# Gate and up of a gated feed-forward as seven block products, with one PSUM bank for projections and tails

## The chip, the cores and the metric

The kernel runs on one core of one Trainium2 chip. The metric is the device time of one execution in microseconds; the number given for a kernel is the median of several executions. A profile is one execution recorded by the hardware profiler; its span runs from the first to the last instruction. Engines: PE is TensorE (matmul; PEld its weight loads), DVE is VectorE, ACT is ScalarE, POOL is GpSimd, SP issues most of the DMAs. Each engine works off its own instructions in order.

## What is computed

All values are f32. x is [8, 256, 512]; eight batches of 256 tokens, 512 features. First a windowed cross-attention with 32 heads is added (q from context and normed x, k and v from each), then a feed-forward:

```python
x = x + tanh(g_xattn[0]) * attention(layernorm(x), ctx, Wq, Wk, Wv, Wsk, Wsv, Wo)
xt = layernorm(x)                                        # feed-forward from here
topk_p, topk_idx = top_k(softmax(xt @ w_router), 4)      # 128 experts
gate, up = (xt @ w_gate).reshape(T, 8, 256), (xt @ w_up).reshape(T, 8, 256)
basis = silu(gate) * up                                  # 8 bases of 256
mixed = sum over the 4 chosen experts e and the bases k of coeff[e] * mix[e, k] * basis[k]
out = mixed @ w_down + (silu(xt @ shared_w_gate) * (xt @ shared_w_up)) @ shared_w_down
x = x + tanh(g_ffn[0]) * out
```

The down projection is linear, so the kernel sums the experts' mixing weights per token first (one coefficient per token and base) and multiplies by w_down once.

## The kernel before

A batch has four pieces of work, each a Python generator that emits instructions and yields a cost after each step:

- `project` (L253): loads x and context, norms x, transposes it, and computes k, q (four groups of 16 matmuls) and v. Each result goes through a PSUM bank and is evicted by ScalarE (L289, L306, L322).
- `attention` (L329): scores on TensorE (L355, four banks, one for each pair of head groups), bias and maximum on VectorE (L368, "softmax rows" here), exponential on ScalarE (L377), division on GpSimd (L387), 32x32 transposes on VectorE (L395), value matmuls on TensorE (L417) into the rest of the same banks, eviction by ScalarE (L434).
- `tail` (L495), for each half of the tokens: output projection (L504), residual, norm, transposition into hT, router (L528), top-4 selection, coefficients `cf`.
- `feed_forward` (L572): for each of four pieces of two bases and for each half t of the tokens, four matmuls of 512 columns for gate and four for up (L589). Tanh on ScalarE (L600) and an STT on VectorE (L601) make silu, L606 multiplies by up, L611 and L613 add the two bases to `mixed[t]`. VectorE's later part of a piece (`late`) is emitted only after the next piece's gate matmuls. Then come the shared part (L630, four steps), and the down projections (L665, L670).

Order: nothing is scheduled by a planner; the loop `run` (L690) always continues the generator with the smallest virtual time, which advances by the yielded cost times a rate chosen at `start`. So the instructions of attention b+1, projection b+2 and the feed-forward of b alternate on each engine in a fixed order. While b is 0, projections and attention are emitted by hand (L705 to L719).

PSUM has eight banks of 2 KB per partition: four for scores and values (`ps_sc`), one for projections (`ps_pj`), one for tails (`ps_tl`), two for the feed-forward (`ps_gu`). Weights of gate and up are loaded anew for each batch, one piece of two bases (1 MB for gate, 1 MB for up) two pieces ahead (`load_gu`, L237, called after a piece's last matmul at L619 and L659), through SP's queue. Waits between engines are put in by the framework from the tiles that instructions touch.

Of the kernel before, what the change touches and what calls it, by code (L numbers as in the profile page):

```python
# [9 lines left out]
F32 = mybir.dt.float32  # L10
# [18 lines left out]
NK2 = NK // 2  # L29
# [8 lines left out]
def gated_block(  # L38
# [28 lines left out]
    three = ctx.enter_context(tc.tile_pool(name="three", bufs=3))  # L67
    small = ctx.enter_context(tc.tile_pool(name="small", bufs=4))
    PS = bass.MemoryType.PSUM
    ps_sc = ctx.enter_context(tc.tile_pool(name="ps_sc", bufs=4, space=PS))  # L70
    ps_pj = ctx.enter_context(tc.tile_pool(name="ps_pj", bufs=1, space=PS))
    ps_tl = ctx.enter_context(tc.tile_pool(name="ps_tl", bufs=1, space=PS))
    ps_gu = ctx.enter_context(tc.tile_pool(name="ps_gu", bufs=2, space=PS))
# [4 lines left out]
    def load(b):  # L78
        xt = three.tile([P, NT, HID], F32, tag="x", name=f"x_{b}")
        ctT = two.tile([P, NC, T], F32, tag="ctT", name=f"ctT_{b}")  # L80
        nc.sync.dma_start(xt, x[b].rearrange("(t p) d -> p t d", p=P))
        nc.sync.dma_start(ctT, context_t[b].rearrange("(c p) t -> p c t", p=P))
        loaded[b] = xt, ctT
# [6 lines left out]
    load(0)  # L90
# [10 lines left out]
    load(1)  # L101
# [59 lines left out]
    dist = const.tile([P, NW * Q], F32, tag="dist", name="dist")  # L161
# [36 lines left out]
    def other_weights():  # L198
# [11 lines left out]
        nc.sync.dma_start(escale, expert_scale.rearrange("(e o) -> e o", o=1))  # L210
        later["wr"] = weight(w_router, HID, E, "wr", nc.sync)
        load_gu(0)
        load_gu(1)
# [20 lines left out]
    wgu = {}  # L234
    PIECES = NK2 + 1

    def load_gu(i):  # L237
        if i >= B * PIECES:
            return
        k2 = i % PIECES  # L240
        for name, routed, shared in (("wg", w_gate, sw_gate), ("wu", w_up, sw_up)):
            t = two.tile([P, NC, 2 * I], F32, tag=name, name=f"{name}_{i}")
            src = routed[:, k2 * 2 * I : (k2 + 1) * 2 * I] if k2 < NK2 else shared
            nc.sync.dma_start(t, src.rearrange("(c p) n -> p c n", p=P))
            wgu[name, i] = t
# [4 lines left out]
    AFTER, BEFORE = 2.0, 1.6  # L250
    projected = {}

    def project(b):  # L253
        def bank(shape, name):

            pool, tag = (ps_gu, "gu") if b < 2 else (ps_pj, "pj")
            return pool.tile(shape, F32, tag=tag, name=name)

        if b > 1:
            load(b)  # L260
            yield 24.0
# [9 lines left out]
        for t in range(NT):  # L271
            evict = transposed(xnT, xns[t], t, f"x{b}", bank)
            yield AFTER
            evict()
            yield BEFORE


        kT = two.tile([P, 2, 2, T], F32, tag="kT", name=f"kT_{b}")
        pk = bank([P, 2, T], f"pk_{b}")
# [7 lines left out]
        for par in range(2):  # L287
            for s in range(2):
                nc.scalar.activation(  # L289
                    kT[:, par, s, :], pk[:, s, :], AF.Copy, scale=kmask[:, par : par + 1],  # L290
                )
        yield BEFORE
# [3 lines left out]
        for g in range(G):  # L296
            pq = bank([P, T], f"pq_{b}_{g}")
# [10 lines left out]
            )  # L308
            yield BEFORE
        projected[b] = kT, qT  # L310


        pv = bank([P, NT, 2, HK * D], f"pv_{b}")
# [11 lines left out]
        )  # L325
        yield BEFORE


    def attention(b):  # L329
# [112 lines left out]
        for u in range(2 * n + 4):  # L442
# [27 lines left out]
            for step, ps in enumerate(((0,), (1, 2), (3,))):  # L470
# [3 lines left out]
                if step == 1 and j == 1 and m is not None:  # L474
                    take(m, scs)
                    if m == n // 4 - 1:
                        start(tail(b, 0, oT), 0.37, total=37.0)
# [11 lines left out]
        start(tail(b, 1, oT), 0.37 if b > 0 else 0.30, total=37.0)  # L489
# [4 lines left out]

    def tail(b, t, oT):  # L495
        def bank(shape, name):
            return ps_tl.tile(shape, F32, tag="tl", name=name)
# [3 lines left out]
        yield 2.0  # L501
        po = bank([P, HID], f"po_{n}")
# [9 lines left out]
        )  # L512
        normed = norm(xt, [t], f"f{b}")
# [5 lines left out]
        hT = hTs[b]  # L519
        evict = transposed(hT, xn, t, f"f{b}", bank)  # L520
        yield 3.0
        evict()
# [241 lines left out]
```

## Time and profile before

| | |
|---|---|
| time, median of 3 | 1091.81 us (1088.89 to 1093.41) |
| profiled execution | 1087.13 us |
| its span | 1085.4 us |
| granted TensorE clock, mean | 0.991 |
| PE busy | 1050.7 us, 97% |
| DVE, ACT, POOL busy | 524.1, 347.2, 228.8 us |
| gate and up matmuls (L589), busy | 465.7 us |
| DMA moved | 120.78 MB |

A line of a group names line, engine, operation, the tile written <- the tiles read, the shape, the number of rows, busy time and mean duration. Each f32 matmul of the code is recorded as two rows. A wait line names who waited for whom: microseconds in total, how often, the longest. A chain line gives start, length and what ran. Busy time of an engine is the union of its rows, so rows that overlap in the pipeline count once; the mean duration of a matmul is longer than the distance of two neighbours.

### The profile page before, as it was taken

Reading aid. Unit: us, or ns where it says so; the run is one execution under the profiler, and the core shown is the slowest. Engines: PE = TensorE matmul, PEld = TensorE weight load, DVE = VectorE, ACT = ScalarE, POOL = GpSimd, SP = SyncE. Lnnn points to the kernel's source line nnn. Section 1 sums busy time; section 2 is a strip of 40 time slices with the busy share of each in tenths; the row PEclk is TensorE's granted clock in tenths of the full one; section 3 lists DMA queues with packets and bytes.
Section 4 is the critical chain, followed back from the end, with each engine's and each line's share of the span. In section 5 each row is a group of like instructions: output and inputs, shape, how many; then the busy total and the mean of one; then the engine's idle time right before and its main releaser. Section 6 shows DMA issues by size and latency. Waiting matters only on the chain.

```text
span 1085.4 us, 23220 instructions
## 1 busy us (share of the span) xinstructions
PE 1050.7 (97%) x9232; PEld 646.2 (60%) x9232; DVE 524.1 (48%) x1952; ACT 347.2 (32%) x1354; POOL 228.8 (21%) x587
## 2 busy tenths in 40 slices
PE   7988999999999999999999999999999999999998
PEld 6765465844658446675566745676455754565445
DVE  1564652536526265353744445444563536663431
ACT  1552442414423134232432224332442314431100
POOL 3342221203212032121312112221221212321000
PEclk9899999999999999999999999999999999999999
DMA  9803421127212462135522254222632236322330
GB/s 304 269 2 78 138 98 57 43 96 216 88 69 71 139 200 79 40 115 127 170 78 78 90 127 156 79 78 89 175 109 77 79 113 166 132 79 99 118 114 19
DMA packets 75132, 120.78 MB, mean 111 GB/s; under 512 B 4624, under 2 KB 27664, under 8 KB 75024
## 3 DMA queue, kind: packets, MB, share of 16 engines
q1 hardware_dynamic: 72912, 117.47, 34.6%
q10 hardware_dynamic: 2112, 1.84, 0.5%
q8 instruction: 72, 1.18, 0.5%
q14 instruction: 36, 0.29, 0.1%
HBM read 98.31 MB, written 4.19 MB: 94 GB/s over the span
## 4 chain that ended last, share of the span: by engine, by line
PE 91%; DVE 6%; ACT 1%; issue 1%; DMA 0%; POOL 0%; DVEq 0%; ACTq 0%
PE gu L589 37%; PE pq L299 10%; PE ps L630 10%; PE sc L417 6%; PE sc L355 6%; PE po L504 5%; PE pd L670 5%; PE pk L282 3%; PE pv L317 3%; PE pd L665 2%; PE pl L528 1%; DVE pt L395 1%; DVE pr L368 1%; ACT pr L377 1%; DVE st_a L115 1%
## 5 line engine op out<-in xcount | busy, mean ns | idle before, releaser
L377 ACT ACTIVATE pr<-pr,nm 128x192 f32<-128x192 f32 (+2 forms) x512 | 218.2, 427 | 475.6 <-DVE rd L384 296.6
L387 POOL TENSOR_SCALAR pr<-pr,rd 128x192 f32<-128x192 f32 (+2 forms) x512 | 205.4, 422 | 582.1 <-DVE rd L384 559.3
L368 DVE CUSTOM_DVE_ANT_1 pr<-sc,nbias 128x192 f32<-128x192 f32 (+2 forms) x512 | 148.8, 324 | 244.4 <-PE sc L355 139.5
L589 PE MATMUL gu<-wu,hT 128*128 128x512 f32 x512 | 232.3, 596 | 1.4 <-DVE th L606 1.4
L589 PE MATMUL gu<-wg,hT 128*128 128x512 f32 x512 | 233.4, 598 | 0.0
L589 PEld LDWEIGHTS gu<-wu,hT 128*128 128x128 f32 x512 | 94.6, 190 | 107.6 <-issue 100.1
L589 PEld LDWEIGHTS gu<-wg,hT 128*128 128x128 f32 x512 | 94.6, 190 | 104.4 <-issue 101.5
L395 DVE STREAM_TRANSPOSE pt<-pr 128x768 f32<-128x768 f32 (+2 forms) x128 | 111.5, 871 | 0.9 <-POOL pr L387 0.8
L601 DVE SCALAR_TENSOR_TENSOR th<-th,gu 128x512 f32<-128x512 f32 x64 | 44.0, 688 | 110.4 <-ACT th L600 110.4
L377 ACT ACTIVATION_READ_ACCUMULATOR pr<-pr,nm 128x1 f32 x512 | 96.1, 188 | 0.0
L417 PEld LDWEIGHTS sc<-pt,vbd 64*32 64x32 f32 x5120 | 61.3, 107 | 25.7 <-issue 20.9
L417 PE MATMUL sc<-pt,vbd 64*32 64x96 f32 (+2 forms) x5120 | 68.8, 231 | 5.0 <-issue 3.0
L355 PE MATMUL sc<-kT,qT 32*128 32x192 f32 (+2 forms) x1024 | 67.4, 342 | 3.0 <-DVE nm L368 2.7
L355 PEld LDWEIGHTS sc<-kT,qT 32*128 32x128 f32 x1024 | 47.6, 187 | 33.1 <-issue 22.3
L299 PE MATMUL pq<-ctT,wq 128*128 128x256 f32 x256 | 61.4, 383 | 2.8 <-ACT qT L306 2.8
L299 PE MATMUL pq<-xnT,wq 128*128 128x256 f32 x256 | 61.9, 385 | 0.0
L606 DVE TENSOR_TENSOR th<-th,gu 128x512 f32<-128x512 f32 x64 | 43.1, 673 | 37.9 <-PE gu L589 37.7
L630 PE MATMUL ps<-hT,wg 128*128 128x256 f32 x256 | 61.2, 382 | 0.0
L630 PE MATMUL ps<-hT,wu 128*128 128x256 f32 x256 | 60.5, 379 | 0.0
L504 PE MATMUL po<-wo,oT 128*128 128x512 f32 x128 | 58.2, 597 | 1.9 <-DVE cf L567 1.9
L299 PEld LDWEIGHTS pq<-ctT,wq 128*128 128x128 f32 x256 | 47.9, 190 | 19.4 <-issue 8.6
L670 PE MATMUL pd<-sd,shT 128*128 128x512 f32 x128 | 58.3, 597 | 0.3 <-DVE shT L643 0.3
(96 smaller groups left out, 880.9 us busy)
## 6 DMA issues: line engine op xcount, KB each, us to landing
wg<-in_L_ffn_w_gate SPq DMA_DIRECT2D x32, 1024.0 KB, 4.9
wu<-in_L_ffn_w_up SPq DMA_DIRECT2D x32, 1024.0 KB, 5.0
vbd<-vpad SPq DMA_DIRECT2D x128, 128.0 KB, 3.2
wg<-in_L_ffn_shared_w_gate SPq DMA_DIRECT2D x8, 1024.0 KB, 5.0
wu<-in_L_ffn_shared_w_up SPq DMA_DIRECT2D x8, 1024.0 KB, 5.4
x<-in_x SPq DMA_DIRECT2D x8, 512.0 KB, 3.8
ctT<-in_ctx SPq DMA_DIRECT2D x8, 512.0 KB, 5.1
out<-x SPq DMA_DIRECT2D x16, 256.0 KB, 2.1
```

The lines of the kernel that those rows point to most:

```text
L299: nc.tensor.matmul(pq, lhsT=wq_sb[:, c, g * P : (g + 1) * P], rhs=(ctT if c < NC else xnT)[:, c % NC, :], start=(c == 0), stop=(c == 2 * N ...
L355: nc.tensor.matmul(seen(scs[p][:, j * COLS : (j + 1) * COLS], qb), lhsT=qT[rows, qb].rearrange("p g q -> p (g q)"), rhs=kT[rows, par, :, f ...
L368: nc.vector.tensor_tensor_reduce(out=part, in0=seen(scs[p][:, j * COLS : (j + 1) * COLS], qb0 + j), in1=bass.AP(tensor=bias.tensor, offset ...
L377: nc.scalar.activation(part, part, AF.Exp, bias=nmax[:, p : p + 1], scale=-1.0, accum_out=den[:, p : p + 1],)
L387: nc.gpsimd.tensor_scalar(part, part, rden[:, p : p + 1], 1.0, op0=ALU.mult, op1=ALU.mult)
L395: nc.vector.transpose(pt[:, u % 4].rearrange("p c (s k) -> p (c s) k", s=2)[:, :, lo:], pr.rearrange("p c (s k) -> p (c s) k", s=2)[:, :, ...
L417: nc.tensor.matmul(scs[gp][32 * c : 32 * (c + 1), 2 * COLS + lo * Q : 2 * COLS + hi * Q], lhsT=vbd[rows, kb % (P // Q), kb // (P // Q) * 2 ...
L504: nc.tensor.matmul(po, lhsT=oT[:, ch // 2, ch % 2, t * P : (t + 1) * P], rhs=wo_sb[:, ch % 2, ch // 2, :], start=(ch == 0), stop=(ch == 3),)
L589: nc.tensor.matmul(gate if up is None else up, lhsT=hT[:, c, t * P : (t + 1) * P], rhs=w_sb[:, c, :], start=(c == 0), stop=(c == NC - 1),)
L601: nc.vector.scalar_tensor_tensor(out=th, in0=th, scalar=1.0, in1=gate, op0=ALU.add, op1=ALU.mult)
L630: nc.tensor.matmul(pg[:, j, :], lhsT=wgu[name, i][:, c, ic * P : (ic + 1) * P], rhs=hT[:, c, :], start=(c == 0), stop=(c == NC - 1),)
L670: nc.tensor.matmul(po, lhsT=shT[:, ic, t * P : (t + 1) * P], rhs=later["sd"][:, ic, :], start=False, stop=(ic == NSI - 1),)
```

## The change

For batches 1 to 7, gate and up of one base are computed together. With tokens split in halves (A, rows of the left matrix), features split in halves (the sum over 512), and B the 512 x 512 matrix whose left columns are the base's gate weights and whose right columns are its up weights, the product is a 2 x 2 by 2 x 2 block product. Strassen's scheme in Winograd's form takes seven block products of (128 tokens) x (256 features) x (256 columns), each two matmuls of 256 columns, for eight. It needs sums of blocks of tokens, sums of blocks of weights, and sums of results:

- Token sums: `token_sums`, four VectorE rows for each batch, issued in the tail.
- Weight sums: batch 0 multiplies as before (`plain`, in halves of gate and up for one base), and GpSimd makes the sums of the weights meanwhile (`weight_sums`, `last_sum`). SP stores blocks and sums in DRAM (`scratch`), from which later batches load seven blocks of 256 KB a base, two bases ahead.
- Result sums: partly in PSUM by accumulation. ScalarE copies the first product into another bank (`seeded`), and later products add to it; the rest is added by VectorE (`second_up`, `rest`). `seeded` is one bank of two halves, used in turn by even and odd bases; `pair0` and `pair1` hold a base each. A matmul at the start of the run writes all of `seeded` once.
- Bases are staggered: 1 and 5 of base k, then 7 of base k-1, 2 and 6 of base k, 3 and 4 of base k-1. The last base's rest lies within the shared part's first step.
- `mixed` and the silu rows are now of 256 columns, one for each base and half. Shared weights are loaded in two parts, and mixed's transposes for both halves go through one bank.
- Projections, tails and `mixed`'s transposes use one bank (`ps_one`) with a flag `held`: a generator that wants the bank while another has it yields until it is free. Batch 0 and 1 project through the pairs.
- The context tile and `prob` have one buffer, context is loaded later; the rates and costs of the generators are other ones, and attention of the next batch starts 0.15 batch earlier.

```diff
+    pair = [ps_gu.tile([P, 2, T], F32, tag=f"pair{j}", name=f"pair{j}") for j in range(2)]
+    seeded = ps_gu.tile([P, 2, T], F32, tag="seeded", name="seeded")
...
+    def hold():
+        while held[0]:
+            yield 0.4
+        held[0] = True
...
+        loaded[1] = x_1, load_context(1)
         later["wr"] = weight(w_router, HID, E, "wr", nc.sync)
-        load_gu(0)
-        load_gu(1)
+        for i in range(2):
+            for g in range(1, 5):
+                load_gu(i, g)
...
+        elif b == 0:
+            src = (w_gate, w_gate, w_up, w_up)[g - 1]
+            rows = slice(HALF, HID) if g in (2, 4) else slice(0, HALF)
+            nc.sync.dma_start(
+                t[:, 0], src[rows, k * I : (k + 1) * I].rearrange("(c p) n -> p c n", p=P)
+            )
+        else:
+            nc.sync.dma_start(t, scratch[k, g])
+
+    def after(i, g):
+
+        b, k = divmod(i, PIECES)
+        if g < 3:
+            load_gu(i + 2, g)
+        else:
+            load_gu(i + 2 if k < NK - 2 else (b + 1) * PIECES + k - NK + 2, g)
...
+        sT = one.tile([P, 4, NC // 2, P], F32, tag="sT", name=f"sT_{b}")
+        a11, a12 = hT[:, : NC // 2, :P], hT[:, NC // 2 :, :P]
+        a21, a22 = hT[:, : NC // 2, P:], hT[:, NC // 2 :, P:]
+        nc.vector.tensor_add(sT[:, 0], a21, a22)
+        nc.vector.tensor_sub(sT[:, 1], sT[:, 0], a11)
+        nc.vector.tensor_sub(sT[:, 2], a11, a21)
+        nc.vector.tensor_sub(sT[:, 3], a12, sT[:, 1])
...
+        def weight_sums(k):
+
+            w = [wgu[k, g] for g in range(1, 5)]
+            nc.gpsimd.tensor_sub(w[0][:, 1], w[2][:, 0], w[0][:, 0])
+            nc.gpsimd.tensor_sub(w[1][:, 1], w[3][:, 0], w[0][:, 1])
+            nc.gpsimd.tensor_sub(w[3][:, 1], w[1][:, 0], w[1][:, 1])
+            for g in (1, 2, 4):
+                nc.sync.dma_start(scratch[k, g], w[g - 1])
+
+        def last_sum(k):
+
+            w = [wgu[k, g] for g in range(1, 5)]
+            nc.gpsimd.tensor_sub(w[2][:, 0], w[3][:, 0], w[2][:, 0])
+            nc.sync.dma_start(scratch[k, 3], w[2])
...
+            for k, t in order:
+                plain(k, t)
+                while len(todo) > 1:
+                    todo.pop(0)()
+                while len(ths) > 3:
+                    mix_in(*next(iter(ths)))
+                if t == 0:
+                    weight_sums(k)
+                yield 3.46
+                if t == 1:
+                    last_sum(k)
+                    for g in range(1, 5):
+                        after(k, g)
...
+            def product(k, m, dst, first=False):
+                g, j = weights_of[m]
+                w = wgu[b * PIECES + k, g]
+                for c in range(NC // 2):
+                    nc.tensor.matmul(
+                        dst, lhsT=sides_of[m][c], rhs=w[:, j, c, :],
+                        start=(first and c == 0), stop=(c == NC // 2 - 1),
+                        skip_group_check=True,
+                    )
+
+            def one_and_five(k):
+                banks[k] = next_pair()
+                product(k, 1, banks[k][:, 0, :], first=True)
+                product(k, 5, banks[k][:, 1, :])
+                after(b * PIECES + k, 1)
+
+            def seed(k):
+                nc.scalar.copy(seeded[:, k % 2, :], banks[k][:, 0, :])
+                ups[k] = three.tile([P, I], F32, tag="up", name=f"up_{b}_1_{k}")
+                nc.scalar.copy(ups[k], banks[k][:, 1, :])
+
+            def two_and_six(k):
+                product(k, 2, banks[k][:, 0, :])
+                product(k, 6, seeded[:, k % 2, :])
+                after(b * PIECES + k, 2)
+
+            def first_gate(k):
+                us[k] = two.tile([P, I], F32, tag="u", name=f"u_{b}_{k}")
+                nc.scalar.copy(us[k], seeded[:, k % 2, :])
+                ths[k, 0] = silu2(banks[k][:, 0, :], f"th_{b}_0_{k}")
+
+            def seven(k):
+                product(k, 7, seeded[:, k % 2, :])
+                after(b * PIECES + k, 3)
+
+            def second_up(k):
+                nc.vector.tensor_add(ups[k], ups[k], seeded[:, k % 2, :])
+
+            def three_and_four(k):
+                product(k, 3, banks[k][:, 1, :])
+                product(k, 4, seeded[:, k % 2, :])
+                after(b * PIECES + k, 4)
+
+            def rest(k):
+                up = three.tile([P, I], F32, tag="up", name=f"up_{b}_0_{k}")
+                nc.vector.tensor_add(up, us.pop(k), banks.pop(k)[:, 1, :])
+                ths[k, 1] = silu2(seeded[:, k % 2, :], f"th_{b}_1_{k}")
+                nc.vector.tensor_mul(ths[k, 0], ths[k, 0], up)
+                nc.vector.tensor_mul(ths[k, 1], ths[k, 1], ups.pop(k))
+
+
+            for k in range(NK):
+                one_and_five(k)
+                if k > 1:
+                    for t in range(NT):
+                        mix_in(k - 2, t)
+                yield 1.73
+                seed(k)
+                if k > 0:
+                    seven(k - 1)
+                    yield 0.86
+                    second_up(k - 1)
+                two_and_six(k)
+                yield 1.73
+                first_gate(k)
+                if k > 0:
+                    three_and_four(k - 1)
+                    yield 1.73
+                    rest(k - 1)
...
         for b in range(B):
+            if b + 1 < B:
+                run(b + EARLY)
+                start(attention(b + 1), 0.86, at=b + EARLY, total=71.0)
             run(float(b) if b > 0 else -0.1)
-            start(feed_forward(b), b + 1.0 - now[0], total=80.5)
-            if b + 1 < B:
-                start(attention(b + 1), 0.90, at=b + 0.01, total=71.0)
+            start(feed_forward(b), b + 1.0 - now[0], total=73.2 if b > 0 else 80.6)
             if b + 2 < B:
-                start(project(b + 2), 0.73, at=b + 0.005, total=71.0)
+                start(project(b + 2), 0.62, at=b + 0.01, total=60.0)
```

`silu2(gate, name)` is a tanh of 256 columns on ScalarE and an STT on VectorE, (tanh + 1) * gate; `mix_in(k, t)` is one VectorE row of 256 columns, which adds a base to `mixed[t]`.

## The prediction

> **What bounds the kernel now.** I read the page's busy shares first, then a table of stages, then the chain that ended last, then TensorE's waits.
>
> ```profile
> PE 1050.7 (97%) x9232; PEld 646.2 (60%) x9232; DVE 524.1 (48%) x1952; ACT 347.2 (32%) x1354; POOL 228.8 (21%) x587
> ...
> PE 91%; DVE 6%; ACT 1%; issue 1%; DMA 0%; POOL 0%; DVEq 0%; ACTq 0%
> ```
>
> ```profile
> 533.00:666.00 133.00, 131.85 (x1232) 81.13 (x1230) 66.50 (x248) 43.56 (x171) 27.75 (x69) 1.00 0.36 113
> ```
>
> TensorE is busy 97% of the span and 131.85 of 133 us in the middle (columns: length, then PE, PEld, DVE, ACT, POOL, clock, DMA share, GB/s). The chain is 91% TensorE. A batch takes 130.4 us (the same stretch of shared products starts at 469.66, 600.03, 730.53 and 860.93 us in the chain). The granted clock is 1.00 there, so clock explains nothing. Only less TensorE work, or more TensorE waiting, moves the time. Two stretches of the chain give the pitch of a matmul:
>
> ```profile
> 1022.56 34.44 PE gu L589 x80
> 1056.99 6.91 PE ps L630 x32
> ```
>
> 80 rows of 512 columns in 34.44 us are 0.430 us each, 32 rows of 256 columns in 6.91 us 0.216 us each (each f32 matmul of the code is two rows). Half the columns cost half the time, so small blocks lose nothing by themselves: the weight load, 190 ns, still fits under 216. The mean durations of 598 and 382 ns on the page are latencies of overlapping rows and may not be multiplied.
>
> What a wait without any cover costs is seen in the list of TensorE's waits:
>
> ```profile
> PE pq L299 <- ACT qT L306: 2.8, 6, 0.5
> ...
> PE po L504 <- DVE cf L567: 1.9, 6, 0.3
> ```
>
> These are the places where nothing stands on TensorE between a matmul and the next use of its bank: 0.47 us behind a 256-column ScalarE eviction of 0.38 us, 0.3 us behind a VectorE row of 0.22. A bare round trip is thus the row plus 0.1 us. Elsewhere a gate bank has at least eight rows of 512 columns (3.44 us) before its reuse.
>
> **Removed: matmul time.** A base of a batch was 16 rows of 512 columns, 16 x 0.430 = 6.89 us. Seven products of two matmuls are 28 rows of 256, 28 x 0.216 = 6.05. That is 0.84 us for each of 8 x 7 = 56 bases, **-47 us** (6.7 a batch). Batch 0 keeps its matmuls, only cut in halves: 0. Clock and the other products stay.
>
> **Added work off TensorE.** Per base: ScalarE three copies and two tanh of 256 columns (5 x 0.374, L638) for one tanh of 512 (0.583), 1.3 us more; VectorE eight 256-column rows (four with a bank 0.42, four with two SBUF inputs 0.50, from L639 and L613), 3.7 us, for half of 2 x (0.688 + 0.673 + 2 x 0.50), 2.4; and four token sums of 0.45 a batch. VectorE goes from 66 to some 78 us, ScalarE from 44 to 54, of a batch of 124-130. Neither becomes the bound by its sum, so the throughput price is 0. DMA: seven blocks of 256 KB a base instead of 1 MB; the share goes from 0.36 to about 0.6 and the loads start two bases ahead (some 28 us against 5 us to landing): 0.
>
> **Added: waits in each base.** This decides. A base's sequence is: products 1, 5; ScalarE copies into the seed bank and out of the pair; product 7 of the base before; 2, 6; 3, 4 of the base before. The three banks allow no spare, and seven() waits for seed() although it writes the other half: in the changed order every product in the seed bank carries a wait on the last ScalarE or VectorE access to that bank. By address there would be no such wait and the sum would stay near -47 us. [...] I go by the order. [...]
>
> A bare wait (0.47 us) fits under the 0.86 us of one product. It is the FIFO ahead of the releaser that doesn't fit. Its pitches:
>
> ```profile
> 405.11 0.33 DVE L368 CUSTOM_DVE_ANT_1 pr<-sc,nbias 128x192 f32<-128x192 f32 x1
> ...
> 405.36 0.35 DVE L368 CUSTOM_DVE_ANT_1 pr<-sc,nbias 128x192 f32<-128x192 f32 x1
> ...
> 405.64 0.68 DVE L606 TENSOR_TENSOR th<-th,gu 128x512 f32<-128x512 f32 x1
> 406.36 1.21 DVE L613 SCALAR_TENSOR_TENSOR mixed<-th,cf,mixed 128x256 f32<-128x256 f32 x2
> 407.48 0.35 DVE L368 CUSTOM_DVE_ANT_1 pr<-sc,nbias 128x192 f32<-128x192 f32 x1
> ```
>
> ```profile
> 550.42 0.46 ACT L377 ACTIVATE pr<-pr,nm 128x192 f32<-128x192 f32 x1
> ...
> 550.87 0.44 ACT L377 ACTIVATE pr<-pr,nm 128x192 f32<-128x192 f32 x1
> ```
>
> Read the starts: softmax rows follow each other at 0.28 us, and already now a softmax row stands 1.8 us behind the FFN's burst (405.64 to 407.48). In the changed order rest() puts five rows at once (STT, two products, two mixes: 0.34 + 4 x 0.40 = 1.95 us) ahead of the softmax rows of heads 1 to 3; their exponentials (0.445 us pitch, by two neighbours on ScalarE) stand ahead of seed()'s copy on ScalarE, and TensorE needs that copy after only products 1 and 5 (1.72 us) plus what lies between. Walked through the order in one middle batch, base by base (us):
> - start of base 3: product 1 waits for rest()'s first row, which on VectorE stands behind one softmax row that needs the value matmuls issued just before, a reciprocal and two projection norms: 0.1 + 0.26 + 0.17 + 2 x 0.50 + 0.4 = 1.95, no cover: **1.95**.
> - seven() in base 3: burst 1.95, three softmax rows to 2.85, exps, two oT copies and the copy to 4.45, against 1.72: **2.75**.
> - base 4: first row of rest() behind a transpose of 0.97: **0.7**; seven(): copy at 4.3 after product 1's start, cover 1.72 + half a pk 1.72: **0.9**.
> - base 1: seven() behind scores, softmax and exp **0.8**; base 2: first row of rest() behind STT and softmax rows **0.5**, seven() **0.2**; base 0: second copy and pair **0.75**.
> - bases 5 to 7: a q projection or value matmuls (1.7 us each) stand in the gap: **0.3** in all.
> - one bank for projections and tails: a router product directly behind hT's eviction **0.6**, others **0.3**.
>
> Sum 9.75; the six bare waits on L306 and L567 of before, 0.8 a batch, go away with the new order. **+8.9 a batch, six batches: +53 us.** While TensorE waits, the two engines empty their queues, so a stall isn't paid twice in a row; it moves later scores and values by as much, and nothing that ends sooner waits for those. Bounds: if VectorE and ScalarE are mostly ahead of the order I walked, only the bare shortfalls remain, 4 a batch; if every base pays like bases 3 and 4, 15.
>
> **Last batch**, without attention: seven() waits for a bare copy, 0.5 x 8 = **+4** (2 to 6).
>
> **Batch 0: weight sums.** Four GpSimd subtractions of 512 elements a base. No row of before is a wide two-input one; from L387 (365 ns at 64, 439 at 192 elements) a one-input row would be 0.62 us. [...] **+4** (0 to 12). Start: less weight traffic in the first 54 us and a later context load behind batch 0's values: **0** (-3 to 3).
>
> **Sum.** -47 + 53 + 4 + 4 = +14. The profiled execution took 1087.1 us (span 1085.4, 1.7 around it): 1101; it lies 4.7 under the median 1091.8, so **1106** against that median.
>
> **Rivals.** (1) The waits are mostly covered: 4 a batch, -47 + 19 + 3 + 2 = -23, **1069**. For it: VectorE is idle half the span, and the 1.7 us waits are lined up with projections. Against: idle VectorE time lies before the burst, not in it. It ends on the other side by one mechanism, the FIFO ahead of seed()'s copy, and decides where the waits of a batch come to less than 6.4 us (6 x (6.4 - 0.8) + 8 - 47 = -5.5). (2) Every base pays, 15 a batch: -47 + 85 + 5 + 8 = +51, **1143**. For it: no base has a spare bank, and shifted attention work can take away the gaps that bases 5 to 7 live on. (3) The first batch's DRAM round trip holds TensorE in each of six bases by 5 us: +30 on the sum, **1136**. [...] (4) The work saved isn't saved, blocks of 256 columns bound by weight loads: refuted by the 0.216 us pitch.
>
> **How the numbers follow.** Likeliest case 0.45 (own range 1086 to 1126), covered 0.30, every base 0.17, round trip 0.08. The time is that of the likeliest, 1106. 8 in 10: from 1066 (the lowest tenth, inside rival 1) to 1142 (the highest, in rivals 2 and 3). A measurement tells about 0.5%, 5.5 us: faster 0.30 (rival 1), slower 0.58 (the rest of the likeliest, 2 and 3), same 0.12, the likeliest case's low end.
>
> **What would show it.** TensorE's busy time near 1004 us plus or minus 8, and its idle time up from 35 to 90-100; in the list of waits the seed bank on ScalarE's seed copies and the pair on VectorE's first row of rest(), 1 to 3 us each, in the bases named; rows of products at 216 ns pitch. Steady batches of about 132 us mean the likeliest case, 127 rival 1, 138 rival 2. Wrong it would be if the waits of product 7 stay under 0.5 us each, or if batch 0 grows by more than 12 us.

## The result and the profile after

The changed kernel takes **1169.03 us** (median of 4 executions, 1168.79 to 1170.87), the kernel before 1091.62 (four executions, 1088.89 to 1093.41): a ratio of 1.0715, interval 1.069 to 1.074. The prediction, 1106, had the direction; the 77 us lie outside its range, which ended at 1142. The profiled execution took 1169.0 us with a span of 1167.2, 81.8 longer than the span before (1085.4).

The page of the changed kernel, with busy times, granted clock in 40 slices, and the chain's shares:

```profile
PE 1040.7 (89%) x10034; PEld 801.5 (69%) x10034; DVE 585.1 (50%) x2220; ACT 410.3 (35%) x1578; POOL 269.3 (23%) x619
...
PEclk9897899998999989999999999999999899999999
...
PE 73%; DVE 13%; ACT 9%; issue 3%; DMA 1%; SPq 0%; POOL 0%; ACTq 0%; DVEq 0%; POOLq 0%
```

TensorE's busy time fell by 10 us, not by 47, and its idle time rose from 34.7 to 126.5. The chain that was 91% TensorE is now 73%; VectorE and ScalarE hold 22% of it. Neither is busy for much more than half the span. They hold it because TensorE waits for single rows of theirs.

The halved blocks do run at half the price. In the chain, in the last batch, where attention no longer interferes:

```profile
1100.30 0.86 PE pair L779 x4
1102.03 1.82 PE pair L779 x8
1104.28 1.13 PE seeded L779 x4
```

Four rows of 256 columns take 0.86 us, 0.216 each, as read from before. But where product 7 waits for the bare copy, between the eight rows and the next four, more is lost than the wait. At the pitch the eight would be done at 1103.76; the next product starts at 1104.28, 0.52 later, and its four rows take 1.13 us, 0.27 over their pitch. A bare wait thus costs 0.8 us, while TensorE's idle time in this stage is 3.8 us for 8 of them, some 0.5 each: the rest is in the rows around the wait and counts as busy.

I cut both traces at the end of each batch's last down matmul. Lengths in us:

| stage | before | after | difference | TensorE idle, before, after | clock, before, after |
|---|---|---|---|---|---|
| start and batch 0 | 233.2 | 259.1 | +25.9 | 22.7, 35.3 | 0.96, 0.93 |
| batch 1 | 135.5 | 139.2 | +3.7 | 2.2, 11.6 | 1.00, 0.98 |
| batch 2 | 130.9 | 138.5 | +7.6 | 1.2, 10.9 | 1.00, 0.98 |
| batch 3 | 130.4 | 138.5 | +8.1 | 1.1, 12.3 | 1.00, 0.99 |
| batch 4 | 130.5 | 136.9 | +6.4 | 1.2, 10.3 | 1.00, 0.99 |
| batch 5 | 130.4 | 142.5 | +12.1 | 1.2, 14.4 | 1.00, 0.98 |
| batch 6 (no projection left to run) | 109.5 | 129.1 | +19.6 | 1.4, 24.1 | 1.00, 0.99 |
| batch 7 (no attention either) | 81.1 | 79.6 | -1.5 | 0.0, 3.8 | 1.00, 1.00 |

Two of these stages of the kernel before, then three of the changed kernel, as the windows have them (columns as in the prediction's window):

```profile
0.00:233.20 233.20, 210.53 (x2186) 144.61 (x2187) 106.87 (x441) 84.95 (x333) 63.29 (x172) 0.96 0.40 123
890.90:1000.40 109.50, 108.11 (x1035) 60.26 (x1035) 62.59 (x236) 38.78 (x158) 26.71 (x69) 1.00 0.39 121
```

```profile
0.00:259.10 259.10, 223.76 (x2355) 176.11 (x2355) 121.97 (x494) 89.94 (x359) 104.81 (x210) 0.93 0.56 173
536.80:675.30 138.50, 126.23 (x1254) 97.68 (x1254) 73.00 (x279) 52.16 (x200) 27.88 (x69) 0.99 0.49 149
954.70:1083.80 129.10, 104.95 (x1116) 77.11 (x1117) 68.39 (x255) 43.96 (x174) 25.54 (x64) 0.99 0.43 138
```

A middle batch is not the 132 of the forecast but 137 to 138.5. More than half of the 82 us (45.5) lie in batch 0 and batch 6, stages that lack the mix of work of the middle; for them I had 4 and 2.

TensorE's waits (who, for whom, us in total, times, longest):

```profile
PE seeded L779 <- ACT seeded L792: 33.0, 29, 3.6
PE pair L779 <- DVE up L820: 18.9, 19, 1.9
...
PE seeded L779 <- ACT u L803: 8.0, 7, 1.5
PE pc L670 <- ACT selT L665: 6.4, 7, 2.3
PE sc L498 <- DMA vbd<-vpad: 6.0, 8, 1.2
PE pl L630 <- ACT hT L163: 5.8, 7, 1.3
```

The first two are the ones named in the forecast: the seed bank on product 1's copy, the pair on the first row of `rest()`. Base 3 of batch 2 shows them one behind the other, on TensorE:

```profile
423.19 1.13 PE L779 MATMUL seeded<-w,hT 128*128 128x256 f32 x4 [1.48 <-ACT u L803]
424.25 0.89 PE L498 MATMUL sc<-pt,vbd 64*32 64x96 f32 x64
427.02 1.38 PE L779 MATMUL pair<-w,hT 128*128 128x256 f32 x4 [1.88 <-DVE up L820]
428.20 1.91 PE L779 MATMUL pair<-w,sT 128*128 128x256 f32 x4
431.23 2.08 PE L779 MATMUL seeded<-w,sT 128*128 128x256 f32 x4 [1.11 <-ACT seeded L792]
```

and on ScalarE, where the copy of 0.37 us that product 7 needs stands behind exponentials and two oT copies:

```profile
429.16 0.46 ACT L458 ACTIVATE pr<-pr,nm 128x192 f32<-128x192 f32 x1 [2.69 <-DVE nm L449]
...
430.05 0.41 ACT L515 COPY oT<-sc 128x128 f32<-128x128 f32 x2
430.35 0.46 ACT L458 ACTIVATE pr<-pr,nm 128x192 f32<-128x192 f32 x1
...
430.80 0.37 ACT L792 COPY seeded<-pair 128x256 f32<-128x256 f32 x1
```

Two of these three waits are in the walk of the prediction: 1.95 us were forecast for the pair, 1.88 measured; 2.75 for product 7, here 1.11, and 2.21 in batch 3. The wait on the copy into u (1.48) is not in it. Nor are the second and third product after it: four rows in 1.91 and 2.08 us instead of 1.03. The window over them says why:

```profile
428.00:433.00 5.00, 3.89 (x9) 2.53 (x9) 2.30 (x9) 2.32 (x10) 0.18 (x1) 0.50 0.32 103
```

The granted clock is 0.50. Read in steps of 1 us over the whole trace, the clock is either full or half, and a dip is one, two or three stretches of about 3.4 us, each of which takes 1.7 us of matmul time. Before has 4 dips that sum to 10 us, all of them in batch 0's stage; the changed kernel has 12 that sum to 34. In batches 2, 3 and 4 they start at 427.8, 571.1 and 704.2 us: at the waits of base 3 each time, but not at the same one. In batch 3 the waits of 1.47 and 1.88 us pass at full clock, and the dip begins after product 7's wait of 2.21.

The starts of all 12 dips lie on one grid: their distances are multiples of 3.413 us, within 0.01 (42 of them from 427.8 to 571.1, 39 to 704.2). In the step of the grid before these three starts TensorE was busy 45, 42 and 45% of the time. In batch 3 the waits of 1.47 and 1.88 us fall into two different steps, busy 57 and 58%, and no dip follows. A limit cannot be read from this: in batch 6 a step at 43% (1031.9 us) brought none.

### The profile page after: what moved, and what is told of

Its sections match the earlier page's. It is cut to its first block, busy times and chain, and to the rows that moved or that the text cites. A ratio compares the mean times of both kernels' runs of the same rounds, so it can differ in the third digit from the quotient of the medians.

```text
span 1167.2 us, 26066 instructions
## 1 busy us (share of the span) xinstructions
PE 1040.7 (89%) x10034; PEld 801.5 (69%) x10034; DVE 585.1 (50%) x2220; ACT 410.3 (35%) x1578; POOL 269.3 (23%) x619
## 3 DMA queue, kind: packets, MB, share of 16 engines
q8 instruction: 79, 1.29, 0.5%
## 4 chain that ended last, share of the span: by engine, by line
PE 73%; DVE 13%; ACT 9%; issue 3%; DMA 1%; SPq 0%; POOL 0%; ACTq 0%; DVEq 0%; POOLq 0%
PE seeded L779 12%; PE pair L779 11%; PE pair L862 10%; PE pair L909 7%; PE pq L377 6%; ACT pr L458 5%; PE sc L498 5%; PE sc L436 5%; PE po L600 4%; PE pair L715 4%; DVE pr L449 3%; PE pair L377 2%; PE pv L397 2%; DVE th L685 2%; DVE mixed L704 1%
## 5 line engine op out<-in xcount | busy, mean ns | idle before, releaser
L779 PE MATMUL seeded<-w,sT 128*128 128x256 f32 x448 | 120.9, 393 | 33.2 <-ACT seeded L792 33.0
L779 PE MATMUL pair<-w,hT 128*128 128x256 f32 x448 | 122.0, 396 | 24.6 <-DVE up L820 18.9
L862 PE MATMUL pair<-hT,w 128*128 128x256 f32 x512 | 122.1, 391 | 1.5 <-DVE up L820 1.5
L779 PEld LDWEIGHTS seeded<-w,sT 128*128 128x128 f32 x448 | 80.5, 192 | 58.0 <-ACT seeded L792 45.8
L779 PE MATMUL pair<-w,sT 128*128 128x256 f32 x448 | 118.2, 387 | 0.0
L779 PEld LDWEIGHTS pair<-w,hT 128*128 128x128 f32 x448 | 82.8, 193 | 46.1 <-DVE up L820 25.4
L476 DVE STREAM_TRANSPOSE pt<-pr 128x768 f32<-128x768 f32 (+2 forms) x128 | 111.4, 871 | 1.3 <-POOL pr L468 1.3
L862 PEld LDWEIGHTS pair<-hT,w 128*128 128x128 f32 x512 | 98.3, 196 | 18.7 <-issue 3.3
L779 PEld LDWEIGHTS pair<-w,sT 128*128 128x128 f32 x448 | 84.9, 193 | 12.8 <-issue 1.4
L779 PE MATMUL seeded<-w,hT 128*128 128x256 f32 x224 | 58.6, 384 | 8.0 <-ACT u L803 8.0
L715 PE MATMUL pair<-w,hT 128*128 128x256 f32 x256 | 62.6, 402 | 3.1 <-DVE th L723 3.1
L909 PE MATMUL pair<-sd,shT 128*128 128x512 f32 x128 | 60.1, 593 | 0.0
```

Of the source, the lines that this page charges most:

```text
L476: nc.vector.transpose(pt[:, u % 4].rearrange("p c (s k) -> p (c s) k", s=2)[:, :, lo:], pr.rearrange("p c (s k) -> p (c s) k", s=2)[:, :, ...
L715: nc.tensor.matmul(pg[:, j, :], lhsT=hT[:, c, t * P : (t + 1) * P], rhs=(lower if c < NC // 2 else upper)[:, 0, c % (NC // 2), :], start=( ...
L779: nc.tensor.matmul(dst, lhsT=sides_of[m][c], rhs=w[:, j, c, :], start=(first and c == 0), stop=(c == NC // 2 - 1), skip_group_check=True,)
L862: nc.tensor.matmul(pg[:, j, :], lhsT=w[:, c, ic % 2 * P : (ic % 2 + 1) * P], rhs=hT[:, c, :], start=(c == 0), stop=(c == NC - 1),)
L909: nc.tensor.matmul(po, lhsT=lhsT, rhs=rhs, start=(j == 0), stop=(j == len(inner) - 1))
```

## Experiments

Each was timed beside the kernel before, with medians of that kernel between 1089 and 1094 us. Stage lengths come from the profiles.

### 1. The copy first

```diff
                 one_and_five(k)
+                seed(k)
                 if k > 1:
                     ...
                 yield 1.73
-                seed(k)
```

> seed()'s two ScalarE copies are emitted directly behind products 1 and 5, ahead of the exponentials that attention emits in the gap. Theory Q (product 7 waits because of what stands ahead of the copy in ScalarE's queue): TensorE's waits of the seed bank on the copies fall from 33.0 us to 15 or less (bare waits of at most 0.5 us each), time 1145 to 1155 us. Rival D (the round trip itself, bank by bank, sets the wait, whatever the queue): the waits stay within 5 us of 33 and the time within 5 us of 1169. Rival C (the loss sits in matmul time and clock): time within 5 us of 1169 too, but the waits fall.

**1135.4 us** (1130.3 to 1140.4; ratio 1.039, 1.027 to 1.051). In the list of waits, product 7's wait shrinks and the others stand:

```profile
PE pair L779 <- DVE up L820: 19.0, 19, 1.9
...
PE seeded L779 <- ACT seeded L792: 7.7, 17, 0.5
PE seeded L779 <- ACT u L803: 7.6, 7, 1.4
```

33.0 became 7.7 us, and no wait is over 0.5: that is the bare copy, as theory Q had it, with a larger gain than it forecast. The middle batches fall to 132.3 to 132.6 us at a clock of 1.00, batch 6 only to 124.5, with a clock of 0.96. So a copy of 0.37 us in the wrong place of a queue cost some 34 us (29 to 39 by the two executions): 25 of it as waiting.

### 2. The burst later

The two products and the two mixing rows that `rest()` and the next base issue together were moved later, behind products 2 and 6, into `multiply`; the first row of `rest()` is written in place into u.

```diff
             def rest(k):
                 ...
-                nc.vector.tensor_mul(ths[k, 0], ths[k, 0], up)
-                nc.vector.tensor_mul(ths[k, 1], ths[k, 1], ups.pop(k))
...
                 two_and_six(k)
+                if k > 1:
+                    multiply(k - 2)
                 yield 1.73
```

> rest()'s two multiplications and the two mixes are emitted half a base later, behind products 2 and 6 of the base after next, so that VectorE's run behind products 3 and 4 is two rows and not six. Theory Q: softmax rows and exponentials come up to 1.6 us earlier, waits of the seed bank on the copies fall from 33.0 to about 22 us, those of the pair on VectorE's up stay near 19, time 1155 to 1160. Rival D: within 5 us of 1169.

**1164.3 us** (1163.2 to 1165.4; ratio 1.0655): a gain of 5, where rival D had at most 5 and theory Q 9 or more.

```profile
PE seeded L779 <- ACT u L803: 20.1, 14, 2.7
PE pair L779 <- DVE u L820: 19.3, 19, 1.9
PE seeded L779 <- ACT seeded L792: 18.3, 23, 2.1
```

The wait on product 1's copy fell by 15 us, more than theory Q asked for, and that on the next copy (u, L803) rose by 12. The move mostly changed which of the two copies is waited for.

### 3. Both

> Both changes of order together. Theory Q: waits of the seed bank on the copies at most 12 us, time 1135 to 1148. Rival D: within 5 us of 1169.

**1146.9 us** (1145.6 to 1148.2; ratio 1.050), inside theory Q's range, but 11 more than with the copy first alone. The wait on product 1's copy is 7.7 us again, but that on u stays at 19.8: with the copy first, moving the burst only does harm.

### 4. Without the copy

```diff
-                nc.scalar.copy(seeded[:, k % 2, :], banks[k][:, 0, :])
```

This leaves out the copy of product 1 into the seed bank, so that the other three blocks lack its term.

> Leaves out the ScalarE copy of product 1 into the seed bank (the products then add to what stands there); all matmuls, weights, VectorE rows and the other copies stay. Theory Q: the 33 us of waits on this copy vanish and half to all of them are gained, time 1135 to 1152. Rival D: the wait goes to the next hand-off in the chain (copy out of the pair, u, up), time above 1158. In both, if matmul time is what I took it for, TensorE's busy time falls to 1020 or less with the breaks; if it stays near 1040 the busy time has another cause (clock, start of each run of rows).

**1133.5 us** (1131.1 to 1135.8; ratio 1.037): no more than with the copy first. Up to batch 6 nearly all of its cost was that of its place: batches 2 and 3 take 132.0 us, batch 6 125.6. In batch 7, where every bare wait on the copy is exposed, leaving it out saves 5.1 us (74.5, with the copy 79.6). TensorE's busy time stays at 1036.2 us, where I had expected 1020 or less. By the rule that I had set, busy time has another cause than these waits: the clock or the start of each run of rows. The mean clock is 0.973 here and 0.971 in the changed kernel.

### 5. Everything first

Experiment 1, and the same for the other three rows that TensorE waits for: VectorE's difference of products 7 and 1 (`second_up`), ScalarE's copy into u (`save`, so far in `first_gate`), and the first row of `rest()` (`first_up`, now written in place into u):

```diff
                 if k > 0:
                     seven(k - 1)
+                    second_up(k - 1)
                     yield 0.86
-                    second_up(k - 1)
                 two_and_six(k)
+                save(k)
                 yield 1.73
                 ...
                     three_and_four(k - 1)
+                    first_up(k - 1)
                     yield 1.73
```

> Every step that TensorE's next product waits for is emitted directly behind the product that it needs: the scalar engine's copy of product 1, VectorE's difference of products 7 and 1, the scalar engine's copy of the gate sum into u, and VectorE's first row of the up sum. Theory Q (the waits are FIFO order: the copy or the sum stands behind work of other generators): the waits of TensorE on product 1's copy fall from 33.0 to about 8 us as with the copy alone, those on the difference of products 7 and 1 from 18.9 to 5 or less, those on the u copy stay below 8; total 1115 to 1125 (the copy alone gave 1135). Rival R (the rest of these waits is the bare chain of product, PSUM pass and next product, about half a microsecond each, whatever the order): the waits on the difference stay at 12 or more, total 1130 to 1140. Neither theory gives back the whole of the 77 us: the start of batch 0 stays some 25 us longer than before.

**1133.7 us** (1133.1 to 1134.2; ratio 1.040, 1.037 to 1.043), within rival R's range, and 1.7 below the copy first alone, which is inside the spread of that one's two executions.

```profile
PE pair L779 <- DVE u L821: 11.2, 13, 1.2
PE sc L436 <- DVE nm L449: 8.7, 10, 1.2
...
PE seeded L779 <- ACT seeded L792: 8.1, 17, 0.9
PE pv L397 <- ACT prob L641: 7.7, 5, 1.6
```

The sum's wait fell from 19.0 to 11.2, between what Q and R had said. But the softmax maxima (3.9 us in the changed kernel) now stand behind the rows put first, and the value projection behind the tail's probabilities (5.0). A middle batch is 133.1 us, 0.8 above experiment 1; batch 6 gains 7.2. Theory Q was right for ScalarE's copy of product 1. For VectorE's rows it was not: in a middle batch what they gain others wait for.

### 6. The second context load last

```diff
-        loaded[1] = x_1, load_context(1)
         later["wr"] = weight(w_router, HID, E, "wr", nc.sync)
         ...
         later["sd"] = weight(sw_down, SI, HID, "sd", nc.sync)
+        loaded[1] = x_1, load_context(1)
```

> The second context load stands behind the loads of the weights and not ahead of them on SP's queue. Theory S (the single context buffer makes SP stand until batch 0's value projection, and the block-diagonal loads of batch 0's attention start late behind it): TensorE's waits on the vbd loads fall from 6.0 us to below 1, batch 0's stage from 259.1 to about 251, total about 1161. Rival (the start is late because of the loads themselves, or what is gained is waited for at the next place): batch 0's stage stays within 3 us of 259, total 1166 to 1171.

**1161.6 us** (1160.0 to 1163.3; ratio 1.066). SP's queue in the changed kernel, and with this edit:

```profile
32.62 0.38 SPq L104 DMA_DIRECT2D ctT<-in_ctx  x1
40.13 4.30 SPq L531 DMA_DIRECT2D vbd<-vpad  x6
```

```profile
33.35 0.37 SPq L104 DMA_DIRECT2D ctT<-in_ctx  x1
34.91 10.73 SPq L531 DMA_DIRECT2D vbd<-vpad  x16
```

There is one context buffer now, so the second context load stands on SP until batch 0's value matmuls have read the first (14.1 us, `SPq L104 <- PE pair L397`). In the changed kernel the weight loads stand behind it, and the block-diagonal loads of batch 0's attention behind those. With the edit the waits on vbd are gone and the first feed-forward product of batch 0 starts at 103.94 us instead of 112.56 (before 96.32). Of the 7.6 us that remain, 6.5 are scores of batch 1 and an output projection (97.48 to 103.94), which before ran behind that product: reordered work, no loss. Batch 0's stage falls by 11.5 to 247.6. Of this, the span keeps 5.7 and the median 7.4: in the profiled execution batch 6, which the edit does not touch, has five dips where the changed kernel's profile has one, a clock of 0.93, and takes 137.9 us instead of 129.1.

### 7. Without the weight sums

```diff
-                if t == 0:
-                    weight_sums(k)
                 yield 3.46
                 if t == 1:
-                    last_sum(k)
```

Left out: the sums and their stores. The later batches load as many bytes of the plain weights.

> Leaves out the weight sums: GpSimd adds nothing in batch 0, nothing is stored to DRAM, and the later batches load the same number of bytes of the weights where the sums would be (the values are not those of the reference). Theory W (the sums and their trip through DRAM delay batch 0 and the first products of batch 1): batch 0's stage falls by 8 us or more, or batch 1's by 3 or more, total 1155 to 1160. Rival (they are hidden, and batch 0 is longer for its start and its waits alone): both stages within 3 us, total 1166 to 1172.

**1157.9 us** (1155.6 to 1160.2; ratio 1.062). Batch 0's stage is 247.6 us again, but the gain lies elsewhere: its first product starts at 112.43, as in the changed kernel, and from there to the end of batch 0 it takes 135.2 us instead of 146.5. The two gains are of different stretches, 8.6 and 11.3 us. GpSimd's sums reach VectorE, as its mixing row shows; this is the row in that stretch, of the changed kernel and without the sums:

```profile
L704 DVE SCALAR_TENSOR_TENSOR mixed<-th,cf,mixed 128x256 f32<-128x256 f32 x14 | 8.9, 652 | 0.0
```

```profile
L708 DVE SCALAR_TENSOR_TENSOR mixed<-th,cf,mixed 128x256 f32<-128x256 f32 x14 | 6.4, 477 | 0.0
```

The same row is 175 ns slower on average: nine of the 14 still take 0.47 to 0.48 us, the other five 0.71 to 1.57. Each of the five starts while GpSimd runs a subtraction, none of the nine does; the one of 1.57 us starts at 178.92, beside subtractions that run from 177.72 to 180.21. Rows with one input in PSUM (`th<-th,pair`) take 420 ns in both kernels, also beside a subtraction (163.10, in one that runs from 162.98 to 164.25).

Two rows of another kind are slower too, the normalization of x for the next projection (L148), with one tensor in SBUF as input: 1.34 us on average beside the sums, and 0.52 to 0.66 in the ten from 290 us on, after the last sum. VectorE is busy for 78.95 us in the stretch, against 72.60 in that of experiment 11, which has no sums either; how much of the 6 us reaches TensorE the runs do not show.

### 8. The kernel before, with one bank

Projections of batches 2 and later, tails and mixed's transposes take turns in it as in the changed kernel; the other bank stays unused.

```diff
-    ps_pj = ctx.enter_context(tc.tile_pool(name="ps_pj", bufs=1, space=PS))
-    ps_tl = ctx.enter_context(tc.tile_pool(name="ps_tl", bufs=1, space=PS))
+    ps_one = ctx.enter_context(tc.tile_pool(name="ps_one", bufs=1, space=PS))
+    held = [False]
...
-                        start(tail(b, 0, oT), 0.37, total=37.0)
+                        start(tail(b, 0, oT), 0.30, total=37.0)
```

> The kernel before with one part of the change alone: projections and tails of batches 2 and later take turns in one PSUM bank, with the changed kernel's rates of the tails; dense products as before. My working put the one bank at 0.9 us a batch, about 5 in all: total 1097. Rival B (the one bank costs more, since the projections and tails run later and in lumps: TensorE's waits on the router's and the projections' copies were 17 us in the changed kernel): 1105 to 1112. Rival C (there is always other work between): 1090 to 1094.

**1121.3 us** (1120.0 to 1122.6; ratio 1.029, 1.026 to 1.032): +31 us, far above each theory. Its waits, and one of them in time, first as before and then with one bank:

```profile
PE pq L318 <- DVE x L532: 10.3, 6, 1.7
...
PE pm L691 <- ACT prob L566: 8.7, 6, 1.4
```

```profile
448.71 3.60 PE L504 MATMUL po<-wo,oT 128*128 128x512 f32 x8
452.14 1.89 PE L299 MATMUL pq<-ctT,wq 128*128 128x256 f32 x8
```

```profile
459.01 3.60 PE L527 MATMUL po<-wo,oT 128*128 128x512 f32 x8
462.54 0.93 PE L377 MATMUL sc<-kT,qT 32*128 32x192 f32 x16
465.19 1.99 PE L318 MATMUL pq<-ctT,wq 128*128 128x256 f32 x8 [1.72 <-DVE x L532]
```

With two banks a q projection stood between the output projection and its residual row, as cover. With one, it is the next user of the bank and waits for that row. Both waits of the list are there six times, 3.2 us for each pair. The stages of batches 2 to 5 take 136 to 137 us instead of 130.5, batch 1 4.1 more, batch 0 6.2 more, and batches 6 and 7, where no projection is left, nothing.

### 9. Batch 6 dense

```diff
+    DENSE = (0, 6)
...
-        elif b == 0:
+        elif b in DENSE:
             src = (w_gate, w_gate, w_up, w_up)[g - 1]
...
-        if b == 0:
+        if b in DENSE:
```

> One part undone in one batch: batch 6, whose stage has no projections of a later batch to put between the products, takes the plain dense loop of batch 0 (with the plain weights loaded again); all else as changed. Theory N (batch 6 is 20 us longer because nothing lies between its products, so that every wait of the chain is bare): its stage goes from 129.1 back to 109 to 112, that of the others stays, total 1149 to 1152. Rival (it is longer for the shared bank or for what the other engines do then): its stage stays at 118 or more, total 1158 to 1165.

**1144.0 us** (1141.2 to 1146.7; ratio 1.050): 25 faster.

```profile
949.30:1060.70 111.40, 107.37 (x1147) 83.45 (x1147) 63.44 (x239) 36.69 (x149) 25.01 (x64) 1.00 0.36 117
```

Batch 6 is back at 111.4 us, in theory N's range. With fewer matmuls to run it had taken 17.7 more. Batch 5's stage is also 3.9 shorter (138.6 instead of 142.5, at a clock of 1.00 instead of 0.98), which puts the total below the forecast of 1149 to 1152.

### 10. The kernel before, with the new rates alone

The second hunk of experiment 8 without the first (and its like for the other half).

> Control for the kernel before with one bank (1121): the kernel before with its two banks, and only the changed kernel's rates of the tails (0.30, 0.31 and 0.26 of a batch where it had 0.37, 0.37 and 0.30). If the bank itself costs the 31 us: 1088 to 1096. If it is the tails' hurry: 1110 or more.

**1089.6 us**, ratio 1.0009 (0.9999 to 1.0019): the 31 us of experiment 8 come with the shared bank, the turns that its users take included, and not with the rates.

### 11. Stores without sums

```diff
-            nc.gpsimd.tensor_sub(w[0][:, 1], w[2][:, 0], w[0][:, 0])
             ...
             for g in (1, 2, 4):
-                nc.sync.dma_start(scratch[k, g], w[g - 1])
+                for a in range(2):
+                    nc.sync.dma_start(scratch[k, g][:, a], w[g - 1][:, 0])
```

All four subtractions are left out; plain weights are stored and loaded in the place of the sums.

> Leaves out GpSimd's weight sums alone: batch 0 stores the same bytes to DRAM (plain weights twice, in more and smaller transfers), and the later batches load them (the values are not those of the reference). Theory G (batch 0's 11 us for the sums come from GpSimd's passes, beside which VectorE's rows are slower: the mixing row 652 ns with the sums, 477 without): first dense product to the end of batch 0 falls from 146.5 to 137 or less, mixing row below 500 ns, total 1157 to 1160. Rival D (they come from the stores and the order of SP's queue): it stays at 143 or more, total 1166 to 1170.

**1165.8 us** (1163.6 to 1168.1; ratio 1.070). The stretch from the first product to the end of batch 0 is 139.9 us and the mixing row 477 ns. Against 146.5 with all and 135.2 with nothing, GpSimd's passes are 6.6 of the 11.3 us, and 4.7 remain with the stores (which were more and smaller ones here); neither theory's number was met. The total shows less than the stage, since batch 6 again runs at 0.94 (135.8 us).

### 12. The three put together

Experiments 1, 6 and 9 in one kernel.

> What helped put together: product 1's copy emitted first, second context load last on SP, batch 6 dense. If the gains add (34 for the copy, of which 4.5 lay in batch 6; 8.5 for the context; 18 for batch 6): 1169 - 29 - 8 - 18 = 1113 to 1117. If they overlap (what one frees, another takes): 1125 or more. Below 1092, that is faster than the kernel before: not expected, since the one bank and the weight sums stay.

**1116.6 us** (1115.2 to 1118.0; ratio 1.0244, 1.021 to 1.028): the gains add. The middle batches are at 133.7 to 134.0 us. It is still slower than before, by 28.1 us of span: 12.7 in batch 0, 0.9 in batch 1, 2.8 to 3.5 in each of batches 2 to 5, 2.0 in batch 6. That the bank alone cost about as much (32.8) is no explanation, since it lay elsewhere: 6.2 in batch 0 and 5.1 to 6.7 in each of batches 2 to 5.

## Why the prediction was wrong

The sign was right. The size was not: four steps of the sum failed, batch 6 taken for a middle batch, the start put at 0, the weight sums put at 4 us, and the middle batches, where a wait was charged with its idle time alone, the clock was taken as unchanged, and the one bank was put at 0.9 us.

Experiment 8 splits the change in two: the bank alone makes the span 32.8 us longer, and the block products with all that they bring add 49.0 to that. By stage, the second part is the changed kernel against experiment 8: batch 0 +19.7, batch 1 -0.4, batches 2 to 5 +2.5, +2.5, +1.0, +5.4, batch 6 +19.9, batch 7 -1.6. Set beside the steps of the prediction (the two parts of batch 0 by experiments 7 and 6):

| step | predicted | measured | error |
|---|---|---|---|
| one bank (0.9 a batch, six batches), on the kernel before | +5.4 | +32.8 | +27.4 |
| batches 1 to 5: -6.7 and the other waits, +1.3 each | +6.5 | +11 | +4.5 |
| batch 6, counted as one of these | +1 | +20 | +19 |
| batch 7: -6.7 + 4 | -3 | -2 | +1 |
| batch 0: sums and their trip through DRAM | +4 | +11 | +7 |
| start | 0 | +9 | +9 |
| sum | +14 | +82 | +68 |

The first two rows hold for this order of the two steps. The changed kernel's own stages divide the same time otherwise. Its batches 1 to 5 are 37.9 us longer than before, for which the prediction had 11. TensorE's idle time there rose by 52.6 us, of which the walk had 44.7; its busy time fell by 14.7, where 33.5 were to go. So 18.8 us of the error in these batches are busy time that the prediction left out. Half clock accounts for up to 12.4 of them (half of TensorE's busy time in the dips there). And the costs of the bank and of the block products don't simply add: with one bank, experiment 1's middle batch takes 132.3 us, less than the 136.0 of experiment 8 with dense products. Which of the two made the changed kernel's middle batches long thus stays open. The generators' other rates and the earlier start of attention were not undone in the changed kernel.

- **Matmul time removed: right, but not seen as busy time.** The pitch of 0.216 us held. In batches 2 to 4 busy time fell by 2 to 3 us, not 6.7, because what a wait costs beyond its idle time, and half clock, count as busy. In experiment 1, without a dip in batch 2 and with shorter waits, it fell by 5.3.
- **Waits in each base: right as idle time.** 9.75 us were walked; batches 2 to 4 wait 10.3 to 12.3 (1.2 before), mostly at the bases and rows named. Not in the walk is the copy into u, 1.5 us; the waits at bases 4 to 7 came out smaller. What the walk left out is the price of a wait beyond its idle time, 0.3 us in the last batch's chain. Experiments 1 and 4 show the mechanism of the largest waits: the FIFO ahead of a short copy, not the copy. Product 7's wait on the copy into the other half of its bank, which the order has, is in the trace: 1.11 us at base 3 of batch 2, 2.21 in batch 3.
- **"Clock stays": failed.** Some 20 us of the difference are clock: half of TensorE's busy time in the dips, 29.9 us against 10.0 (24 if their idle time counts too). The trace shows half clock (0.50) in stretches of 3.413 us on one grid, and dips where no single wait is as long as such a stretch, in batch 2: 1.48, 0.89 of small value matmuls, 1.88. What sets a dip off was not shown. I had the sum of the waits and did not ask how close together they lie.
- **One bank: mis-sized, by 27 us on the kernel before.** I looked for places where one generator uses the bank twice in a row. I did not ask what the other generator's matmuls had covered while they still had a bank of their own. The changed kernel's own trace lays only 2.5 us a batch directly at the bank (pc, pl and pv). How much two banks would save in it was not tried: scores keep four tiles alive and the products three banks, and with the one bank these are the eight that the kernel before uses too.
- **Batch 6 counted as a middle batch: failed.** The prediction itself let bases 5 to 7 live on projections standing in the gaps. Batch 6 has no projections. Its waits on product 1's copy are 13.4 us of 24.1 us idle, up to 3.6 each. That copy is only a part: without it (experiment 4) the batch still takes 125.6 us. With dense products (experiment 9) it takes 111.4.
- **Start at 0: failed.** The walk had the context load behind batch 0's values, and left out the loads of attention that SP holds behind it: 8.6 us (experiment 6).
- **Weight sums: right in kind, too small.** The +4 was reached with 1.1 us for a sum, a term that no run shows; in the changed kernel a sum took 1.29, and some of VectorE's rows beside it are slower. 4 became 11, of which 6.6 are GpSimd's passes and 4.7 go with the stores (experiments 7 and 11).
- **Rivals.** "Every base pays" came nearest by its number, 1143, but not by its reason: in batches 2 to 4 TensorE's waits sum to 10.3 to 12.3 us, near the 9.75 of the likeliest case and not 15, and half of the error (35 of 68 us) lies in batches 0 and 6. "The waits are mostly covered" is what experiment 1 begins to give (7.9 us of idle in a middle batch instead of about 11), and even then the kernel is slower, with 25 us more in batch 0 and 15 in batch 6.

## What to carry to other kernels

Walk a change through the first and the last stages of a pipeline by themselves: there the work that covers a wait in the middle can be missing, and a queue holds loads that the middle does not have. When two users are put on one buffer, list for each use what stood as cover between a matmul and its eviction, and check whether that cover is now the next user. And emit the short row that the matmul engine needs directly behind its product, before anything else can enter that engine's queue; but on an engine where several such rows meet, as on VectorE here, this may only choose who waits.

## What was not expected of the hardware

- Half clock (0.50) in quanta of 3.413 us on a fixed grid; in the changed kernel's batches 1 to 6 each dip stands behind a single wait of 2.2 to 2.4 us or a pair of 1.5 and 1.9. The same instructions can meet the grid well or badly: batch 6 has one dip in the changed kernel (clock 0.99, 129.1 us) and five in experiment 6, which did not touch it (0.93, 137.9 us). So a gain in one stage can be lost in another.
- A wait costs more than its idle time: about 0.5 us idle make a base 0.8 us longer (6.83 instead of 6.05 us from product to product in the last batch).
- A VectorE row with two SBUF inputs goes from 477 to 652 ns on average beside GpSimd's 1.29 us subtractions: most rows are unchanged, single ones take up to 1.57 us.
